# Two graph-attention and mixture-of-experts layers on one core: where the second early fetch of sums and the first early stores stand in SyncE's queue

## The chip, the cores and the metric

The kernel runs on one core of one Trainium2 chip. The metric is the device time of one execution in microseconds (us); lower is better. Times are medians of several executions. A profile is one further execution, taken by the hardware profiler[...].

Engines are named as in the profile: PE is TensorE, DVE is VectorE, ACT is ScalarE, POOL is GpSimd, SP is SyncE. A letter q behind an engine's name means its sequencer, which issues DMAs, waits on semaphores and takes branches. Each engine works through its own instructions in order. A block, below, is a page of 128 token rows that belong to one expert.

## The reference

The input is `x` (2708 rows of 256 numbers) and an adjacency matrix `adj` (2708 x 2708). There are two layers, each an attention over the graph and then a mixture of experts, both added to their input. What matters here is the very end, the mixture of experts of layer 1:

```python
def _L1_ffn_ref(x, gate_w, gate_b, w1, b1, w2, b2, gamma, beta):
    B, S, H, F, E, K = (8, 4096, 256, 512, 16, 2)
    gate_logits = x @ gate_w + gate_b
    topk_vals, topk_idx = jax.lax.top_k(gate_logits, K)
    topk_w = jax.nn.softmax(topk_vals, axis=-1)
    h = jax.nn.relu(jnp.einsum('bsh,ehf->bsef', x, w1) + b1)
    expert_out = jnp.einsum('bsef,efh->bseh', h, w2) + b2
    sel = jnp.take_along_axis(expert_out, topk_idx[:, :, :, None], axis=2)
    moe = jnp.sum(topk_w[..., None] * sel, axis=2)
    y = x + moe
    ...
    return (y - mu) / jnp.sqrt(var + EPS) * gamma + beta
# layer 1, last step
x = x + _L1_ffn_ref(_layernorm(x)[None], ...)[0]
```

Every row goes to 2 of 16 experts. The two results are weighed, summed with the row, normalised, and added to the layer's input.

## The kernel before

**Tiles and blocks.** The 2708 rows lie in 22 tiles, tiles 0 to 19 of 128 rows and two of 74 rows at the end. For the experts the rows are sorted into blocks. Layer 1 has 45 blocks that are certain to be needed (`SURE1`, numbers 0 to 44) and up to 13 more that stand in a branch, `rest()`, which is taken only if the routing needs them. It is not taken with this input.

**One block** is computed by `Experts.stream`. Its steps, with the lines of the profile:

- `load_w1` (L749) and `load_w2` (L753): SP issues the two weight transfers of the block's expert, 512 KB each. There are three rooms for weights, and block b uses room b % 3: the tiles named `wide_mask` are rooms 0 and 1, the tile named `room` is room 2. A transfer is left out when the room already holds the expert. Such an issue still waits like any other, but takes about 0.08 us in SP's timeline instead of 0.38.
- `fetch` (L765): SP issues the load of the block's 128 rows into `xr`.
- `turn` (L461) and the copy to `lo` (ACT, L1007): the rows are transposed.
- `hide` (PE, L880, 8 matrix products in 16 records) fills `hid_ps` from w1; `bend` (ACT, L884, 4 times) applies the relu into `ht`.
- `weigh`: DVE forms `side` (L872), ACT forms the weight `w` (L874).
- `sum_hidden` (PE, L898) fills `out_ps` from `ht` and w2; PE does it for block b after `hide` of block b+1.
- `scaled` (DVE, L902 and L904) multiplies by the weight into `yo`; `add` (POOL, L909) is an indirect DMA that adds the rows onto `sums1[b % 2]` in DRAM. An add waits until the last add on the same half has landed.

**The end of a tile.** When its two sums are complete, they are fetched from `sums1` into `y_all` (the profile calls it `mask_t`, whose room it uses), added, normalised and stored. For tiles 0 to 11 this is done early, beside the last blocks, by `early_last`: the fetch of six tiles from both halves (SP, L1417, two transfers of 768 KB), three additions (POOL, L1947), statistics (DVE, L427 and L428), the reciprocal root (DVE, L368 to L380) and two operations a tile (DVE, L1957 and L1959). Tiles 0 to 5 are ready once blocks below 36 are added, tiles 6 to 11 once blocks below 39 are.

**After the blocks**, all engines come to the branch of `rest()` (L940 and L943). On the path that skips it each sequencer waits for what its engine has issued and then raises the semaphores that the skipped work would have raised; POOL's entry of this kind is `INC_SWDGE_SEM`. Only then can SP issue the fetches of the ten last tiles (`load_y`, L1417 and L1420, eight transfers), because they wait for those semaphores. Then come the stores of tiles 0 to 11 (L2039), and `last1` finishes tiles 12 to 21 (L1981 on PE, L427, L434, L452, L2001, L2005) with their stores (L2007, L2013).

**What sets the order.** Within this stage a planner, `Clock`, runs generator pieces against assumed durations. A piece yields an engine and a time, or a `Mark` that it waits for, and the order in which pieces are resumed is the order in which instructions are written into each engine's queue. `clock.moved` sets a mark from an assumed time of a transfer; `clock.set` sets it to now. The pieces `fetcher` (issues L765) and `loader` (issues L749 and L753) run through all 45 blocks. The planner's times are not the chip's: an instruction that is written early and whose semaphore comes late holds all that stands behind it.

Of the kernel before, what the change touches and what calls it, by code (L numbers as in the profile page):

```python
# [146 lines left out]
def kernel(  # L147
# [25 lines left out]
    nc = tc.nc  # L173
# [11 lines left out]
    tiles = [(t, P if t < TF else TAIL) for t in range(T)]  # L185
# [90 lines left out]
    def of_pair(src, lo, r=P):  # L276

        return src[lo * P:lo * P + 2 * r, :].rearrange("(p s) d -> p s d", s=2)
# [434 lines left out]
    class Experts:  # L713
# [236 lines left out]
        def stream(self, clock, stages, bank, acc, xrs, los, wides, widened, started):  # L950

            NB, FC = self.sure, self.FC
            self.known_at, self.planned_at, self.scattered_at = (
                {upto: Mark() for upto in stages} for _ in range(3))
            self.added_at = [Mark() for _ in range(NB)]
            hidden_at, out_at, xg_at, xt_at, ht_at, w_at = (
                [Mark() for _ in range(NB)] for _ in range(6))
            xr_slots, xts, weights, hidden = {}, {}, {}, {}
            hts = Slots(clock, 2)

            def stage(b):
                return next(upto for upto in stages if b < upto)

            def fetcher():
                for b in range(NB):
                    yield self.known_at[stage(b)]
                    yield self.scattered_at[stage(b)]
                    if b >= 3:
                        yield hidden_at[b - 3]
                    xr_slots[b] = yield from xrs.get()  # L970
                    self.fetch(b)
                    clock.moved(xg_at[b], 0.5, 2.2)

            def loader():
                yield widened
                for b in range(NB):
                    yield self.known_at[stage(b)]
                    if b < 2:
                        room = []
                        for _ in range(2):  # L980
                            yield from wides.get()
                            room.append(wide_tile())
                        self.add_room(b, *room)
                    else:
                        yield started
                        yield hidden_at[b - 2]
                    self.choose(b)
                    self.load_w1(b)
                    clock.moved(Mark(), 1.7, 2.0)
                    if b >= 3:  # L990
                        yield out_at[b - 3]
                    self.load_w2(b)
                    clock.moved(w_at[b], 1.7, 2.0)

            def turn(b):
                yield xg_at[b]
                slot = yield from bank.get()
                ps = ps_tile("tr_ps", self.t_tag)[:, :D].rearrange("p (c n) -> p c n", n=P)
                yield "PE", 0.4
                turn_rows(self.rows[b][:, :D], P, ps)  # L1000
                clock.start(turned(b, ps, slot), 0)

            def turned(b, ps, slot):
                lo_slot = yield from los.get()
                xt = self.xt_tile()
                yield "ACT", 0.4
                nc.scalar.copy(xt, ps)  # L1007
                clock.set(slot)
                xts[b] = xt, lo_slot
                clock.set(xt_at[b])  # L1010

            def relu(b, f, ps, slot):
                yield "ACT", 0.38
                self.bend(b, f, hidden[b][0], ps)
                clock.set(slot)
                if f == FC - 1:
                    clock.set(ht_at[b])

            def weigh(b):
                yield "DVE", 0.2  # L1020
                yield "ACT", 0.3
                weights[b] = self.weigh(b)

            def finish(b, ps, slot):
                yield "DVE", 0.7
                yo = self.scaled(b, ps, weights.pop(b))
                clock.set(slot)
                yield "POOL", 1.6
                self.add(b, yo)
                clock.set(xr_slots.pop(b))  # L1030
                clock.set(self.added_at[b], 4.5)

            def outputs(b):
                slot = yield from acc.get()
                ps = ps_tile("out_ps", self.o_tag)
                yield ht_at[b]
                yield "PE", 2.05
                ht, ht_slot = hidden.pop(b)
                self.sum_hidden(b, ht, ps)
                clock.set(ht_slot)  # L1040
                clock.set(out_at[b])
                clock.start(finish(b, ps, slot), 0)

            def compute():
                yield started
                yield from turn(0)
                due = []
                for b in range(NB):
                    yield self.planned_at[stage(b)]
                    yield xt_at[b]  # L1050
                    yield w_at[b]
                    slot = yield from hts.get()
                    hidden[b] = self.pool.tile([P, FC, P], F32, name="ht", bufs=2), slot
                    xt, lo_slot = xts.pop(b)
                    clock.start(weigh(b), 0)
                    for f in range(FC):
                        slot = yield from bank.get()
                        ps = ps_tile("hid_ps", self.h_tag)
                        yield "PE", 0.47
                        self.hide(b, f, xt, ps)  # L1060
                        clock.start(relu(b, f, ps, slot), 0)
                        if f == 0:
                            clock.set(hidden_at[b])
                    clock.set(lo_slot)
                    due.append(b)
                    if b + 1 < NB:
                        there = xg_at[b + 1].at is not None and xg_at[b + 1].at <= clock.now
                        if there:
                            yield from turn(b + 1)
                        while len(due) > there:  # L1070
                            yield from outputs(due.pop(0))
                        if not there:
                            yield from turn(b + 1)
                    self.beside(b)
                for b in due:
                    yield from outputs(b)

            clock.start(fetcher())
            clock.start(loader())
            clock.start(compute(), 2)  # L1080

# [571 lines left out]
    for k in range(17):  # L1653
# [8 lines left out]
        if k >= 14:  # L1662
            lo = 4 * (k - 14)
# [37 lines left out]
    clock = Clock()  # L1701
# [14 lines left out]
    def small(n):  # L1716

        return "DVE", 0.19 * n
# [202 lines left out]
    def add_to_x(t, r):  # L1921
# [5 lines left out]
    y_all = mask_flat.bitcast(F32)[:, :2 * T * D].rearrange(  # L1927
        "p (k t d) -> p k t d", k=2, d=D)
# [5 lines left out]
    EARLY_LAST = ((tiles[:6], 36), (tiles[6:12], 39))  # L1934
    assert ENDS1[:2] == (6, 12) and list(early1.values()) == [8, 20] and E1 == 16

    def early_last(group, done):

        yield experts1.added_at[done - 1]
        mark, lo, n = Mark(), group[0][0], len(group)  # L1940
        for k in range(2):
            experts1.early_read(k, fetch_rows(y_all[:, k, lo:lo + n], sums1[k], group), done)
        clock.moved(mark, 0.8 * n, 2.5)
        yield mark
        for t in range(lo, lo + n, 2):
            yield "POOL", 1.3
            nc.gpsimd.tensor_tensor(y_all[:, 0, t:t + 2], y_all[:, 0, t:t + 2],  # L1947
                                    y_all[:, 1, t:t + 2], OP.add)
        for t, r in group:
            yield "DVE", 0.63  # L1950
            ln_y.stats(y_all[:, 0, t], t, r)
        yield small(13)
        rsqrt(ts(ln_y.mv[:, lo:lo + n, 1], LN_EPS, OP.add), ln_y.rstd[:, lo:lo + n])
        for t, r in group:
            yield "DVE", 0.95
            y = y_all[:, 1, t]
            nc.vector.scalar_tensor_tensor(y, y_all[:, 0, t], ln_y.mv[:, t, 0:1], last["gamma"],  # L1957
                                           op0=OP.subtract, op1=OP.mult)
            nc.vector.scalar_tensor_tensor(y, y, ln_y.rstd[:, t:t + 1], x1[:, t, :], op0=OP.mult,  # L1959
                                           op1=OP.add)  # L1960

    def load_y(group, mark):
        lo = group[0][0]
# [65 lines left out]
    clock = Clock()  # L2029
# [4 lines left out]
    loads = [Mark() for _ in late_last]  # L2034
    for group, mark in zip(late_last, loads):
        load_y(group, mark)
    for group, _ in EARLY_LAST:
        for (t, _), _ in zip(group[::2], group[1::2]):
            nc.sync.dma_start(of_pair(out, t), y_all[:, 1, t:t + 2])  # L2039
    for group, mark in zip(late_last, loads):  # L2040
        clock.start(last1(group, mark))
    clock.run()
# [31 lines left out]
```

## Time and profile before

| | |
|---|---|
| Median of 3 runs | 1165.3 us (1164.83 to 1167.05) |
| Profiled execution, its own time | 1183.92 us |
| Its span, first to last instruction | 1182.2 us |
| PE busy | 1049.9 us, 89% of the span |
| DVE, ACT, POOL busy | 537.3, 575.6, 367.1 us |
| Mean granted PE clock | 0.944 |
| Moved by DMA | 238.96 MB, 202 GB/s on average |

PE is busy in nearly the whole span, but the 40 slices of the page (29.6 us each) show it at 8, 5 and 3 tenths in the last three: the end of the kernel is a stage with limits of its own. It is this end, from about 1095 us on, that the change touches; so it is read from the timeline, the stages and the chain of that stretch, and not from the busy shares of the whole. "Idle before, and its releaser" in a timeline names the event that came last before the instruction could start.

### The profile page before, as it was taken

To read this page: it belongs to the slowest core of one execution; us is meant where nothing else is said; L and a number is where in the kernel's file an instruction comes from. 1 tells how busy PE (TensorE), PEld (TensorE's weight loads), DVE (VectorE), ACT (ScalarE), POOL (GpSimd) and SP (SyncE) were. 2 spreads that over 40 slices of the span, in tenths; PEclk is the share of its full clock that TensorE was granted. 3 is DMA by queue.
4 is the path that set the end of the run, shared out by engine and by line. 5 is a ranking of instruction groups with operands and counts; after the bars stand their busy time and mean duration, and the time that the engine had idled before them with its cause. 6 is when DMAs were issued, how large, how long until landed. Compare 5 with 4: busy or idle time off the path is not lost. (4 is left out here: it accounts for less than half of the span.)

```text
span 1182.2 us, 21323 instructions
## 1 busy us (share of the span) xinstructions
PE 1049.9 (89%) x6705; PEld 928.9 (79%) x6705; DVE 537.3 (45%) x2073; ACT 575.6 (49%) x1609; POOL 367.1 (31%) x422
## 2 busy tenths in 40 slices
PE   5999999969989999999998999998865698899853
PEld 4888888857879999989998746998865587898742
DVE  7778888856521111110111357367755631122454
ACT  4877677644534444434444475457544244344312
POOL 7611121211242222221224330542540635333432
PEclk9999999988999999999999999998976899899966
DMA  9964554312879999999899689001315457778943
GB/s 282 303 233 147 169 168 150 134 70 66 302 229 317 322 324 323 320 284 331 265 317 363 189 240 285 1 6 50 104 50 181 123 142 180 181 200 206 302 107 120
DMA packets 165053, 238.96 MB, mean 202 GB/s; under 512 B 10627, under 2 KB 139966, under 8 KB 162224
## 3 DMA queue, kind: packets, MB, share of 16 engines
q1 hardware_dynamic: 146116, 214.09, 55.2%
q0 software_dynamic: 18816, 23.42, 10.4%
q8 instruction: 56, 0.92, 0.3%
q14 instruction: 65, 0.53, 0.2%
HBM read 205.54 MB, written 54.99 MB: 220 GB/s over the span
## 5 line engine op out<-in xcount | busy, mean ns | idle before, releaser
L904 DVE TENSOR_SCALAR yo<-out_ps,w 128x256 f32<-128x256 f32 x92 | 44.5, 484 | 416.1 <-PE out_ps L898 408.0
L1235 PE MATMUL att_ps<-g_all,z 128*128 128x257 f32 (+3 forms) x968 | 227.2, 388 | 0.0
L1235 PEld LDWEIGHTS att_ps<-g_all,z 128*128 128x128 f32 (+3 forms) x968 | 177.3, 188 | 36.3 <-issue 9.0
L898 PE MATMUL out_ps<-room,ht 128*128 128x256 f32 x872 | 199.0, 380 | 0.0
L880 PEld LDWEIGHTS hid_ps<-xt,room 128*128 128x128 f32 x1504 | 175.3, 192 | 10.9 <-ACT w L874 4.2
L880 PE MATMUL hid_ps<-xt,room 128*128 128x128 f32 x1504 | 177.3, 276 | 7.1 <-DMA room<-in_L_ffn_W_dram 3.8
L898 PEld LDWEIGHTS out_ps<-room,ht 128*128 128x128 f32 x872 | 161.3, 191 | 20.8
L1221 ACT ACTIVATE zr<-e_bc,minus_one,g_all 128x256 f32<-128x256 f32 (+3 forms) x242 | 130.5, 592 | 58.6 <-DVE z L1224 57.9
L884 ACT ACTIVATE ht<-hid_ps,w_t 128x128 f32<-128x128 f32 x376 | 128.4, 364 | 30.8 <-PE hid_ps L880 8.2
L909 POOL DMA_INDIRECT sums<-yo,xg x43 | 66.9, 1556 | 234.2 <-DVE side L872 178.3
L1635 PE MATMUL att_ps<-half,wide_mask 128*128 128x258 f32 (+1 forms) x968 | 127.0, 293 | 3.9 <-issue 2.4
L674 POOL DMA_INDIRECT rows_d<-xr,place x88 | 91.9, 1044 | 123.7 <-DVE xr L443 77.0
L1635 PEld LDWEIGHTS att_ps<-half,wide_mask 128*128 128x128 f32 (+1 forms) x968 | 124.0, 198 | 5.0 <-issue 2.5
L909 POOL DMA_INDIRECT sums<-yo,xr x45 | 70.7, 1571 | 143.5 <-DMA sums<-yo,xr 37.0
L1224 DVE SCALAR_TENSOR_TENSOR z<-zr,mask_t 128x256 f32<-128x256 f32 (+3 forms) x242 | 96.0, 419 | 30.4 <-ACT zr L1221 16.8
L884 ACT ACTIVATE ht<-hid_ps,w1x 128x128 f32<-128x128 f32 x180 | 61.3, 362 | 97.7 <-PE hid_ps L880 82.0
L874 ACT ACTIVATE w<-xg,side 128x1 f32<-128x1 f32 x43 | 12.7, 294 | 165.9 <-DVE side L872 165.9
L880 PE MATMUL hid_ps<-lo,wide_mask 128*128 128x128 f32 x480 | 67.3, 298 | 15.2 <-DMA wide_mask<-in_L_ffn_w_dram 13.7
L880 PEld LDWEIGHTS hid_ps<-lo,wide_mask 128*128 128x128 f32 x480 | 64.5, 211 | 19.3 <-issue 15.5
L1512 POOL CAST wide_mask<-mask_t 128x1408 fp32r<-128x1408 fp8e4 x31 | 42.6, 1376 | 104.8 <-PE att_ps L1635 70.7
L898 PE MATMUL out_ps<-wide_mask,ht 128*128 128x256 f32 x240 | 61.3, 401 | 0.0
L461 PE MATMUL tr_ps<-ident,xr 128*128 128x128 f32 (+1 forms) x214 | 38.8, 290 | 23.9 <-DMA xr<-rows_d 9.0
(296 smaller groups left out, 1355.7 us busy)
## 6 DMA issues: line engine op xcount, KB each, us to landing
room<-in_L_ffn_W_dram SPq DMA_DIRECT2D x94, 1024.0 KB
wide_mask<-in_L_ffn_w_dram SPq DMA_DIRECT2D x60, 512.0 KB
room<-in_adj_dram SPq DMA_DIRECT2D x20, 1354.0 KB
room<-in_L_ffn_w_dram SPq DMA_DIRECT2D x30, 512.0 KB
rows_d<-nobody SPq DMA_DIRECT2D x1, 7511.0 KB
rows_d<-nobody SPq DMA_DIRECT2D x5, 1295.0 KB
sums<-nobody SPq DMA_DIRECT2D x2, 2944.0 KB
xr<-rows_d SPq DMA_DIRECT2D x45, 129.5 KB
```

Of the source, the lines that this page charges most:

```text
L461: nc.tensor.transpose(ps[:, c, :r], src[:, c * P:(c + 1) * P], ident[:r, :r])
L674: ins = nc.gpsimd.indirect_dma_start(out=self.rows_d[:, :], in_=self.rows[t][:r], in_offset=None, out_offset=bass.IndirectOffsetOnAxis(ap= ...
L880: nc.tensor.matmul(ps[:, :P], w1_b[:, c, f * P:(f + 1) * P], xt[:, c, :], start=(c == 0), stop=(c == DC - 1))
L884: nc.scalar.activation(ht[:, f, :], ps[:, :P], self.func, bias=self.bias[:, f, b:b + 1])
L898: nc.tensor.matmul(ps[:, :D], ht[:, f, :], self.rooms[b % 3][1][:, f, :], start=False, stop=(f == self.FC - 1))
L904: nc.vector.tensor_scalar(yo, ps[:, :D], w, None, op0=OP.mult)
L909: ins = nc.gpsimd.indirect_dma_start(out=self.sums[k][:, :], in_=yo, in_offset=None, out_offset=bass.IndirectOffsetOnAxis(ap=self.rows.pop ...
L1221: nc.scalar.activation(zr[:k, :n], e_bc[:k, lo:lo + n], AF.Relu, bias=minus_one[:k], scale=g_all[:k, j, D + 1:D + 2])
L1224: nc.vector.scalar_tensor_tensor(z[:k, :n], zr[:k, :n], 1.0, mask_t[:k, j // 2, lo:lo + n, j % 2], op0=OP.add, op1=OP.mult)
L1235: nc.tensor.matmul(accs[i][:r, :D + 1], z[:k, q * P:q * P + r], g_all[:k, j, :D + 1], start=(j == 0), stop=(j == LAST))
L1512: nc.gpsimd.tensor_copy(m, src)
L1635: nc.tensor.matmul(accs[i][:, :D + 2], wide_masks[i, j % 2][:k, j // 2, :], half_k[:k, j, :], start=(j == 0 and half_k is halves[0]), stop ...
```

## The change

The fetch of tiles 6 to 11 waits, in the planner, for two new marks: `loaded`, set when the loader has issued the weights of the last block, and `fetched`, set when the fetcher has issued the rows of the last block. The fetch of tiles 0 to 5 stays where it was. Tiles 0 to 5 are stored by the same piece that finishes them, which also waits for the two marks before it issues the three stores; the stores of tiles 6 to 11 stay behind the branch.

```diff
@@ Experts.stream
             self.added_at = [Mark() for _ in range(NB)]
+            self.loaded, self.fetched = Mark(), Mark()
@@ fetcher
                     self.fetch(b)
                     clock.moved(xg_at[b], 0.5, 2.2)
+                clock.set(self.fetched)
@@ loader
                     self.load_w2(b)
                     clock.moved(w_at[b], 1.7, 2.0)
+                clock.set(self.loaded)
@@ early_last(group, done)
         yield experts1.added_at[done - 1]
         mark, lo, n = Mark(), group[0][0], len(group)
+        if lo:
+            yield experts1.loaded
+            yield experts1.fetched
         for k in range(2):
             experts1.early_read(k, fetch_rows(y_all[:, k, lo:lo + n], sums1[k], group), done)
         clock.moved(mark, 0.8 * n, 2.5)
...
             nc.vector.scalar_tensor_tensor(y, y, ln_y.rstd[:, t:t + 1], x1[:, t, :], op0=OP.mult,
                                            op1=OP.add)
+        if not lo:
+            yield experts1.loaded
+            yield experts1.fetched
+            early_out(group)
+
+    def early_out(group):
+        for (t, _), _ in zip(group[::2], group[1::2]):
+            nc.sync.dma_start(of_pair(out, t), y_all[:, 1, t:t + 2])
@@ after the branch
     for group, mark in zip(late_last, loads):
         load_y(group, mark)
-    for group, _ in EARLY_LAST:
-        for (t, _), _ in zip(group[::2], group[1::2]):
-            nc.sync.dma_start(of_pair(out, t), y_all[:, 1, t:t + 2])
+    early_out(tiles[6:12])
```

In the program that comes out of the planner, PE's order is the same as before. The other queues, from the fetch on:

- SP, before: w1 of block 42; fetch of tiles 6 to 11; w2 of 42; rows of 44; w1 and w2 of 43; w1 and w2 of 44; branch; eight late fetches; six stores.
- SP, after: w1 and w2 of 42; rows of 44; w1 and w2 of 43; w1 and w2 of 44; fetch of tiles 6 to 11; three stores; branch; eight late fetches; three stores.
- POOL, before: the additions of tiles 6 to 11 stand between the adds of blocks 40 and 41. After: they stand behind the add of block 44, ahead of the branch.
- DVE, before: statistics, root and final operations of tiles 6 to 11 stand among `yo` of blocks 41 to 44. After: all of them stand behind `yo` of block 44, ahead of the branch. `side` of block 42 stands ahead of the final operations of tile 0 instead of behind those of tile 1.
- ACT: `w` of block 42 stands behind the copy to `lo` of block 43, where it stood ahead of three of the relus of block 42.

## The prediction

> **What bounds the kernel now.** I read the end of the kernel backwards. The chain of work that ended last gives the points that everything hangs on (columns: start, us, what):
>
> ```profile
> 1119.48 26.52 DMA sums<-yo,xr
> ...
> 1146.07 0.39 SPq L1417
> ...
> 1149.54 12.30 DMA mask_t<-sums
> ...
> 1161.89 5.46 PE y_ps L1981 x14
> ```
>
> The first late fetch leaves at F = 1146.07. Behind it the stage is a fixed piece: 12.3 us until the 74-row fetch lands, then products, roots and stores, 36.1 us in all to the span's end at 1182.2. The 26.5 us in front are put down to one add, but they hide the path I need, so I asked for SP's timeline and for that of the engines. SP:
>
> ```profile
> 1110.61 0.37 SPq L749 DMA_DIRECT2D wide_mask<-in_L_ffn_w_dram  x1
> 1113.18 0.96 SPq L1417 DMA_DIRECT2D mask_t<-sums  x2
> 1114.55 0.54 SPq L753 DMA_DIRECT2D wide_mask<-in_L_ffn_w_dram  x1
> ...
> 1118.32 0.38 SPq L749 DMA_DIRECT2D wide_mask<-in_L_ffn_w_dram  x1
> ```
>
> w1 of block 42 at 1110.61, then the fetch of tiles 6 to 11, which waits for the adds of blocks 37 and 38 until 1113.18, then w2 of 42, and only at 1118.32 w1 of block 43. The engines (in brackets: idle before, and who ended it):
>
> ```profile
> 1117.91 1.89 PE L898 MATMUL out_ps<-room,ht 128*128 128x256 f32 x8
> ...
> 1126.68 3.75 PE L880 MATMUL hid_ps<-lo,wide_mask 128*128 128x128 f32 x16 [6.88 <-DMA wide_mask<-in_L_ffn_w_dram]
> ...
> 1133.28 1.95 PE L880 MATMUL hid_ps<-lo,room 128*128 128x128 f32 x16
> ...
> 1137.02 1.89 PE L898 MATMUL out_ps<-room,ht 128*128 128x256 f32 x8
> ...
> 1140.67 1.55 POOL L909 DMA_INDIRECT sums<-yo,xr  x1 [0.91 <-DVE yo L904]
> ```
>
> PE stands 6.88 us before block 43, for that w1. The same 16 records then take 3.75 us instead of 1.95, since the granted clock is 0.50 from 1122 to 1132 (stages of 2 us). So PE loses 6.9 us by the wait, and about 2.8 more by the clock: block 44 starts 6.60 us after block 43, where undisturbed blocks follow each other at 3.84 (1103.49, 1107.34, 1111.18). The last add starts at A = 1140.67, and F follows 5.40 us later. What fills these is in the rows of the branch:
>
> ```profile
> L943 POOLq INC_SWDGE_SEM  x1: 1596/1596/1596, 1144.5 to 1144.5; - x1
> ```
>
> The add lands about 3.8 us after its start, POOL's sequencer then spends 1.6 us raising the semaphores of the work skipped, and SP goes.
>
> [...] w1 of 43, issued 4.2 us behind 1.5 MB of sums and 3.8 behind w2 of 42, landed after 8.3 us. [...] L1957 takes 1.48 us beside POOL's L1947, 0.48 without. [...] the add at 1127.46 does start just when the additions end.
>
> **The change, part by part.**
>
> *The fetch goes behind the weights.* SP is freed of a wait (until 1113.18) and of two issues (0.96). w2 of 42 then waits only for `out_ps` of block 39 (PE done at 1111.34): 1111.4. Steps of SP as now (1.3 us to the rows, 1.8 to the next w1) give rows of 44 at 1112.7 and **w1 of 43 at 1114.5**, 3.8 us earlier, with 0.5 MB of w2 ahead of it instead of 2 MB. Block 38's w1, behind a full queue, took 6.1 us (1091.81 to 1097.9); in a queue that is nearly drained (131 GB/s in 1114 to 1116, 278 before) I estimate 4 to 5: landed by 1119.2. PE is free at 1119.8.
>
> *PE also needs `lo` of 43.* Before, ACT stood at `w` of 42 until DVE reached `side` at 1121.34, so `lo` came at 1122.9; a block 43 with early weights would still have lost 3 us. In the new order that `w` stands behind `lo`, so `lo` is there at about 1118.6. Block 43 starts at **1119.9**.
>
> *From there to the last add.* DVE is busy with tiles 0 to 5 (six times 0.91 us from 1119.7, with L902 and L904 of block 41, 0.64, and two `side`): `side` of 43 at 1123.1, so ACT ends `w` and the last relu of 43 at 1123.9 and `lo` of 44 at 1124.3. Block 44 starts at 1124.4, then 1.95 + 1.85 + 1.9 for itself and two `out_ps`: PE ends at 1130.1 instead of 1138.9. DVE has nothing else queued there (tiles 6 to 11 stand behind), so `yo` starts at 1130.1, and **A = 1130.9** (0.77 us after `yo`, as now). The add of 42, which it must wait for, starts at 1127.0 and lands at 1130.8. A comes 9.8 us earlier.
>
> *The fetch itself* (two issues, 1.5 MB) waits behind w2 of 44, and that for `out_ps` of 41, 1119.8: issued by 1121.0. It took 9 us to its first use before (1114.1 to 1123.15), in a fuller queue; so 1130 at the latest. The first user, POOL, is not free before A + 1.55 = 1132.5. Nothing stands behind it on SP but stores and the branch: no cost.
>
> *Three stores ahead of the branch.* They wait for DVE to end tile 5, 1126, cost SP 3 x 0.4 us, and their 768 KB land by about 1131. SP's part of the branch waits for them, but F comes later. Cost nothing, under cover of the adds; without it 2 to 3 us. Three stores fewer behind F gain nothing: the chain there hangs on the 74-row fetches, at 49 GB/s and a DMA share of 0.13 (1155 to 1157), two of 16 engines; the stores queue behind them.
>
> *Three additions of POOL move between the last add and the branch.* They took 4.15 us before; from A + 1.55 they end at A + 5.75. Does `INC_SWDGE_SEM` wait for them? The trace doesn't show this case. Lower bound: it does not, and F = A + 5.4; a gain is excluded, since nothing leaves POOL's path there. Upper bound: it does, and F = A + 5.75 + 1.6 + 0.1 = A + 7.45. Indirect DMAs do queue behind additions, so I take the upper one: F = 1130.9 + 7.45 = **1138.4, 7.7 us earlier**. Against it: in layer 0 the same operation (started 673.5, 1.49 us) ran beside an add that occupied POOL until 674.4.
>
> *DVE's work on tiles 6 to 11* now follows the additions: 0.53 a tile for statistics, 2.4 for the root, 12 x 0.47 for L1957 and L1959; it ends at about A + 15 = 1146, and holds up the late statistics, which would start 6.9 us after F, at 1145.3. That costs about a microsecond there, hidden: DVE had stood 6.4 us before the 74-row tile (until 1164.76, 18.7 us after F). If the cover were gone it would be 1 to 2.7 us.
>
> **Sum.** 9.8 - 2.1 = 7.7 us. Profiled execution: 1183.9 - 7.7 = 1176.2 us. It stands 18.6 us above the median of the runs (1.6%); the gain is waiting for DMA and PE at half clock, so I take it over unscaled: 1165.3 - 7.7 = **1157.6 us**.
>
> **The rivals.**
> - *POOL's semaphores don't wait for the additions*: all 9.8 us arrive, 1155.5. For it: the overlap in layer 0. [...]
> - *The weights of 43 are late again*: at 8.2 us after issue, as before, they land at 1122.7. PE idles 2.9 us and runs one block at half clock (3.59 instead of 1.95, as after the 1.93 us gap at 1096.0). 4.5 us of the gain go: 1162.1.
> - *Nothing is gained*: something else, the adds' own succession or DVE, holds A to within 2 us of now. Against it: adds of both halves are 3.8 us apart and land in 3.8.
> - *Slower*: POOL becomes the end. The additions run beside DVE's statistics and take the longest value seen, 1.86 us each; then F = A + 1.55 + 5.6 + 1.6 = A + 8.8, 3.4 us worse than now. It decides as soon as A comes forward by less than 3.4 us; with no gain in A, 1168.7. Against it: 6.9 us of idle PE are plain, and what ended them is moved.
> - That the change doesn't do what it says is excluded: the new queue has the weights ahead of the fetch.
>
> **How the numbers follow.** Forecast 0.47; semaphores pass 0.27; weights late 0.12; no gain 0.07; slower 0.07. About 0.2% (2.3 us) is what a measurement of this kernel can tell from no change. The first three lie beyond it: faster 0.86, same 0.08, slower 0.06 (a small part of the slow case lies within). The range goes from 1154.3 (all 9.8 and a microsecond of steps that run closer than I put them) to 1162.2 (weights late).
>
> **What would show it.** In the profile after: no wait of PE for `wide_mask` near block 43, or one under 1 us; clock 1.00 through blocks 43 and 44; w1 of 43 on SP about 3.8 us behind w1 of 42; the last add some 10 us earlier; POOL's L1947 behind it, and the first late fetch 7.4 us after it (5.4 if the semaphores pass); 36 us from there to the end. I am wrong if PE still waits over 2 us there, if the last add moves by less than 5 us, or if the stage behind F gets longer because DVE comes late.

## The result and the profile after

The median fell from 1165.07 us (20 runs) to 1159.62 us (20 runs, 1152.76 to 1166.44). The ratio is 0.9954 with a 95% interval of 0.9932 to 0.9975, that is 5.4 us, between 2.9 and 7.9. Two later sets of runs gave 0.9952 (0.9934 to 0.9971) and 0.9939 (0.9918 to 0.9960). The gain is real; it is somewhat smaller than the 7.7 us of the forecast. Of the executions reported below one, of the kernel with the fetch alone, took 1562.73 us at a granted clock of 0.647; its median and ratio leave that one out.

The profiled execution took 1164.64 us with a span of 1162.9, so the two spans differ by 19.3 us. Most of that has nothing to do with the change: block 38, ahead of everything the change touches, already starts 12.7 us earlier. One profile is one execution. So I compare stages, counted from the start of block 42 on PE, and not ends. A wait just ahead of that point is left out by this, and the first profile of after has one, for w1 of block 41:

```profile
1099.05 3.27 PE L880 MATMUL hid_ps<-lo,room 128*128 128x128 f32 x16 [2.10 <-DMA room<-in_L_ffn_w_dram]
```

The profile of before has no such wait. It is not the stall in a new place, though: waits of 1.0 to 2.4 us ahead of block 41 stand in nine of the fourteen profiles of this document, two of them of kernels with the fetch at its old place.

SP's timeline of the kernel after shows w1 of blocks 42 and 43 (the first two lines), the moved fetch and the three stores:

```profile
1096.22 0.37 SPq L749 DMA_DIRECT2D wide_mask<-in_L_ffn_w_dram  x1
...
1100.12 0.37 SPq L749 DMA_DIRECT2D wide_mask<-in_L_ffn_w_dram  x1
...
1108.78 0.96 SPq L1420 DMA_DIRECT2D mask_t<-sums  x2
1109.85 4.15 SPq L1974 DMA_DIRECT2D out_dram<-mask_t  x3
```

w1 of 43 goes out 3.9 us behind w1 of 42; it was 7.7 us before. In the engines' timeline of the kernel after, blocks 43 and 44 start 3.84 us apart with no wait, at full clock (1.00 from 1103.00 to 1120.07; 1.95 us each):

```profile
1108.45 1.95 PE L880 MATMUL hid_ps<-lo,wide_mask 128*128 128x128 f32 x16
...
1112.29 1.95 PE L880 MATMUL hid_ps<-lo,room 128*128 128x128 f32 x16
...
1114.56 1.54 POOL L909 DMA_INDIRECT sums<-yo,xr  x1 [2.88 <-DVE w L902]
...
1117.95 0.48 DVE L904 TENSOR_SCALAR yo<-out_ps,w 128x256 f32<-128x256 f32 x1 [1.29 <-PE out_ps L898]
1118.12 1.55 POOL L909 DMA_INDIRECT sums<-yo,xr  x1 [2.01 <-issue]
1121.91 1.54 POOL L909 DMA_INDIRECT sums<-yo,xr  x1 [2.25 <-issue]
1122.91 4.27 POOL L1953 TENSOR_TENSOR mask_t<-mask_t 128x512 f32<-128x512 f32 x3
```

The stall is gone. What is new stands in the last four lines: `yo` of 44 starts at 1117.95, but the add that takes it only at 1121.91, 3.96 us later, where it was 0.77. The timeline puts that idle time down to "issue", which names no cause. In the program, this add waits for the landing of the add of block 42 on the same half of the sums. The wait itself is on record with POOL's sequencer (duration in ns: least, median, most; first and last start in us), which stands at a semaphore of L909 from 1117.9 for 3.31 us:

```profile
L909 POOLq EVENT_SEMAPHORE  x1: 3310/3310/3310, 1117.9 to 1117.9; - x1
```

In the trace the landing of an add is 16 updates of its semaphore. Those of the add of block 42 (started at 1114.56) come from 1119.68 to 1121.19, the last 6.6 us behind its start; the sequencer's wait ends at 1121.2 and the last add starts 0.72 us behind the landing. Likewise 43 waits for 41 (1110.13, landed at 1117.39 after 7.3 us) and starts 0.72 us behind it. In the fourteen profiles together, 18 of the adds of blocks 41 to 44 start 0.72 us behind the landing of the add before them on their half: these are the adds that were held by it.

The branch's row for POOL's sequencer in the kernel after (columns as above):

```profile
L943 POOLq INC_SWDGE_SEM  x1: 1596/1596/1596, 1125.5 to 1125.5; - x1
```

POOL's sequencer begins to raise the semaphores at 1125.5, while the three additions of POOL (1122.91 + 4.27) still run until 1127.2. What it waited for is the last add: the raising starts 0.02 to 0.03 us behind the landing of that add in all fourteen profiles. The first late fetch leaves at 1127.13, 5.22 us behind the last add.

Followed back from the end, the chain of work that ended last now reaches no further than this (second line: PE on the late tiles):

```profile
1136.47 0.24 issue
1136.71 5.59 PE y_ps L1995 x16
```

and PE's timeline says what it had waited for:

```profile
1136.71 10.77 PE L1995 MATMUL y_ps<-mask_t,ident 128*128 128x256 f32 x40 [18.79 <-DVEq L943]
```

Before, PE began on the late tiles 3.0 us behind the first late fetch and then stood for the 74-row fetches. Now it begins 9.6 us behind it, because DVE, which has the statistics and the twelve final operations of tiles 6 to 11 ahead of the branch, reaches the branch only at 1136.2. From there PE never stops. The stage behind the fetch is 35.8 us, where it was 36.1: the same length, with another cause.

The stages of every profile (one execution each), in us. The first two columns go from start to start of blocks 42, 43 and 44 on PE; A is the last add, F the first late fetch. The kernels of the experiments are described below.

| Kernel | 42 to 43 | 43 to 44 | 44 to `yo` of 44 | `yo` to A | A to F | F to end | 42 to end |
|---|---|---|---|---|---|---|---|
| before | 10.99 | 6.60 | 6.62 | 0.77 | 5.40 | 36.1 | 66.5 |
| after | 3.84 | 3.84 | 5.66 | 3.96 | 5.22 | 35.8 | 58.3 |
| after, second | 3.92 | 3.99 | 5.77 | 3.58 | 5.43 | 35.9 | 58.6 |
| after, third | 3.86 | 4.04 | 5.77 | 3.44 | 5.25 | 36.3 | 58.7 |
| fetch alone | 3.95 | 4.50 | 5.77 | 3.31 | 5.33 | 35.7 | 58.5 |
| stores alone | 11.74 | 6.15 | 6.62 | 0.76 | 5.39 | 34.1 | 64.7 |
| behind w1, stores early | 6.21 | 5.56 | 5.67 | 0.77 | 5.39 | 36.2 | 59.8 |
| behind w1, stores late | 3.84 | 4.05 | 5.77 | 2.17 | 5.27 | 35.4 | 56.5 |
| the same, second | 3.85 | 4.09 | 6.51 | 1.08 | 5.43 | 35.3 | 56.2 |
| the same, third | 3.84 | 4.20 | 6.63 | 1.27 | 5.32 | 35.7 | 57.0 |
| after, an eighth of the bytes | 3.98 | 4.45 | 5.77 | 1.89 | 5.35 | 35.3 | 56.8 |
| before, an eighth | 10.39 | 6.30 | 6.61 | 0.76 | 5.36 | 34.3 | 63.7 |
| engines' order alone | 10.29 | 5.78 | 5.66 | 0.78 | 5.74 | 35.2 | 63.5 |
| engines' order, an eighth | 7.16 | 5.27 | 5.66 | 3.60 | 5.25 | 36.2 | 63.1 |

### The profile page after: what moved, and what is told of

Read it like the earlier page. It is cut to its first block, busy times and chain, and to the rows that moved or that the text cites. A ratio compares the mean times of both kernels' runs of the same rounds, so it can differ in the third digit from the quotient of the medians.

```text
span 1162.9 us, 21320 instructions
## 1 busy us (share of the span) xinstructions
PE 1042.8 (90%) x6705; PEld 925.1 (80%) x6705; DVE 537.8 (46%) x2073; ACT 577.9 (50%) x1609; POOL 367.4 (32%) x422
## 5 line engine op out<-in xcount | busy, mean ns | idle before, releaser
L1224 ACT ACTIVATE zr<-e_bc,minus_one,g_all 128x256 f32<-128x256 f32 (+3 forms) x242 | 130.4, 592 | 58.8 <-DVE z L1227 58.1
L909 POOL DMA_INDIRECT sums<-yo,xg x43 | 66.8, 1554 | 233.9 <-DVE side L872 185.3
L909 POOL DMA_INDIRECT sums<-yo,xr x45 | 70.8, 1574 | 128.6 <-DMA sums<-yo,xr 40.8
L874 ACT ACTIVATE w<-xg,side 128x1 f32<-128x1 f32 x43 | 12.7, 294 | 169.1 <-DVE side L872 169.1
```

The source lines that it names most:

```text
L909: ins = nc.gpsimd.indirect_dma_start(out=self.sums[k][:, :], in_=yo, in_offset=None, out_offset=bass.IndirectOffsetOnAxis(ap=self.rows.pop ...
L1224: nc.scalar.activation(zr[:k, :n], e_bc[:k, lo:lo + n], AF.Relu, bias=minus_one[:k], scale=g_all[:k, j, D + 1:D + 2])
```

## The experiments

They were run in three sets; within a set all kernels and the kernel before ran on the same chip, and only these are compared. The kernel before took 1186.40, 1183.55 and 1164.71 us in the three.

### Which part of the change does it

Fetch alone: the fetch of tiles 6 to 11 is moved, all six early stores stay behind the branch.

```diff
-        if not lo:
-            yield experts1.loaded
-            yield experts1.fetched
-            early_out(group)
...
-    early_out(tiles[6:12])
+    early_out(tiles[:12])
```

> The fetch of tiles 6 to 11 moved as in the changed kernel, all six early stores behind the branch as before. Theory (the moved transfers slow the last adds): the 1.5 MB of sums alone still lie ahead of the adds of blocks 41 and 42, so these land in 5.5 to 7.3 us instead of 3.8; the last add starts 11.5 to 13.5 us behind the start of block 43's hidden products (13.5 in the changed kernel, 10.2 if nothing slowed the adds); time 1157.5 to 1160. Rival (the adds are late for POOL's or DVE's own order): nothing moves, 13.5 us and 1159.6. Second rival (the stores are the harm): adds land in 3.8 us, 10.2 us, 1156.4.

Measured: 1181.46 us, ratio 0.9956 (0.9937 to 0.9975), the gain of the whole change. The last add starts 13.6 us behind block 43. That rules out the second rival, that the stores are the harm, but it doesn't tell the theory (up to 13.5) from the first rival (13.5); this is settled further down.

Stores alone: the fetch stays, the stores of tiles 0 to 5 go ahead of the branch.

```diff
-        if lo:
-            yield experts1.loaded
-            yield experts1.fetched
         for k in range(2):
             experts1.early_read(k, fetch_rows(...), done)
```

> The fetch of tiles 6 to 11 stays at its old place, only the three stores of tiles 0 to 5 go ahead of the branch. Theory: PE's wait of 5 to 7 us before block 43 is back with its half clock behind it, the last add lands in 3.8 us, and the time is that of before, 1164 to 1166. Rival (the three stores carry the gain [...]): 1159 to 1161, and the 74-row fetch lands earlier than 15.8 us behind the first late fetch.

Measured: 1186.43 us, ratio 1.0003 (0.9981 to 1.0025). PE's timeline of this kernel has the stall back, and the last add lands in 3.8 us again:

```profile
1128.83 3.75 PE L880 MATMUL hid_ps<-lo,wide_mask 128*128 128x128 f32 x16 [7.74 <-DMA wide_mask<-in_L_ffn_w_dram]
```

So the gain is the fetch's; the three stores give and cost nothing that can be told from zero (2.3 us under to 3.0 over).

### Does the fetch have to go behind all weights?

Behind w1: the fetch stands behind w1 of block 43 and ahead of its w2; the additions are kept behind all adds. Once with the three stores ahead of the branch, once with all six behind it.

```diff
@@ loader
                     clock.moved(...)
+                    if b == NB - 2:
+                        clock.set(self.w1_out)
@@ early_last
         if lo:
-            yield experts1.loaded
-            yield experts1.fetched
+            yield experts1.w1_out
         for k in range(2):
             experts1.early_read(k, fetch_rows(...), done)
+        if lo:
+            yield experts1.loaded
+            yield experts1.fetched
```

> As the changed kernel, with the orders of PE, DVE, ACT and POOL unchanged; on SP the fetch of tiles 6 to 11 stands behind w1 of block 43 instead of behind w2 of 44. Theory: w1 of 43 is still in time (no wait of PE over 1 us before block 43), the 1.5 MB are through before the adds of 41 to 43 start, these land in 3.8 to 5 us, the last add starts 10.2 to 11 us behind block 43's start instead of 13.5, time 1156 to 1157.5. Rival (POOL's or DVE's own order): 13.5 us and 1159.6 as in the changed kernel. Against both: w2 of 43, now behind the fetch, comes late for its products, PE waits before them, and the time is 1160 to 1163.

> As the kernel with the fetch behind w1 of block 43, and all six early stores behind the branch. Theory: adds land in 3.8 us [...], the last add 10.2 us behind block 43's start, time 1155.5 to 1157. If the stores cost the adds nothing, the same as with them; if they cost 1 us of landing, 1 us below it. Rival (POOL's or DVE's order): 13.5 us, 1159.6.

Measured: 1179.43 us, ratio 0.9940 (0.9915 to 0.9965), and 1178.88 us, ratio 0.9941 (0.9915 to 0.9966). In the first one's profile PE stood 2.1 us ahead of block 43: w1 of 43, with 1.5 MB issued 0.6 us behind it, took 7.3 us to land. It did not stand there in any of the three profiles of the second, where w1 landed in 4.8 to 5.1 us with the same bytes behind it. What made the difference is open. (PE had waited 1.0 to 1.5 us ahead of block 41 in these three and only 0.1 in the first, so SP was further ahead of it by 0.5 to 1.0 us.) The last add waits less in these kernels than in the kernel after (`yo` to A 0.8 to 2.2 us). It stands 12.0 us behind block 43 in both, less than the rivals' 13.5 but more than the theories' 10.2 to 11.

The second form again, beside the kernel after, in two more sets:

> The changed kernel once more, beside the three kernels that run with it on the same chip. Both theories: some 5.4 us under the kernel before (ratio 0.9932 to 0.9975); last add 13 to 13.6 us behind the start of block 43, because the adds of 43 and 44 wait for the landing of the adds of 41 and 42, 7 to 8 us after their start; semaphores raised beside the additions, first late fetch 5.2 to 5.4 us behind the last add.

> The fetch of tiles 6 to 11 behind w1 of block 43, ahead of its w2, all six early stores behind the branch; once more, beside the changed kernel. If the place of the fetch behind w1 is what matters, it lies 1 to 3 us under the changed kernel, since the 1.5 MB of sums have passed before the adds of 42 to 44: last add 10.8 to 12 us behind the start of block 43. Rival: the two are alike, the weights of 44 pay for it (w2 of 43 behind 1.5 MB holds up PE by what the adds save), within 1 us of each other.

> The fetch behind w1 of 43, ahead of its w2, all early stores behind the branch, beside the changed kernel once more. If its place is the better one, 1 to 3 us under the changed kernel again (it was 1.9 under it, with intervals that meet); if the two are alike, within 1 us.

> The changed kernel on the same chip, for the comparison with the fetch behind w1: 5 to 6 us under the kernel before.

Measured: 1177.55 (after) and 1175.69 us (behind w1; ratio to before 0.9931, 0.9912 to 0.9949) in one set, 1158.06 and 1156.07 us (0.9917, 0.9887 to 0.9947; 6 runs) in the other. It was 1.9 and 2.0 us lower. Each pair's intervals meet; both pairs together, resampled, give 1.9 us with a 95% interval that begins at zero (0.0 to 3.8). The kernel after did not run in the first set; there this version lies 2.6 us under the fetch alone, with an interval of 2.3 over to 4.4 under. PE's timeline of the last run shows what it pays:

```profile
1105.85 1.99 PE L899 MATMUL out_ps<-wide_mask,ht 128*128 128x256 f32 x8 [0.60 <-DMA wide_mask<-in_L_ffn_w_dram]
```

In this profile w2 of 43, now behind the 1.5 MB, holds PE 0.6 us (44 to `yo` is 6.6 instead of 5.8), and the adds give back 2.2 (`yo` to A 1.27 instead of 3.44). Of the versions that do all the work this one is probably the best, by 2 us.

### Why the last adds land late

The kernel after with the moved fetch cut to 16 of 128 rows:

```diff
+            if lo:
+                ins = nc.sync.dma_start(y_all[:16, k, lo:lo + n], <rows 0 to 15 of each tile>)
+            else:
+                ins = fetch_rows(y_all[:, k, lo:lo + n], sums1[k], group)
```

> The changed kernel, but the fetch of tiles 6 to 11 brings only 16 of the 128 rows of each tile, an eighth of its bytes, in the same two issues with the same waits (the remaining rows of these tiles are left out). Theory, the 1.5 MB delay the landing of the adds: the adds of 41 and 42 land within 4.5 us, those of 43 and 44 start within 1 us of their yo, the last add stands 10.3 to 11 us behind the start of block 43, and the time is 2 to 3.2 us under the changed kernel. Rival, the order on POOL or DVE (or the three stores, 0.75 MB) sets them: the last add stays 13 us or more behind it and the time within 0.8 us of the changed kernel.

Measured: 1173.48 us (6 runs; ratio 0.9912, 0.9880 to 0.9944), 4.1 us under the kernel after in the same set (1.5 to 8.2; 2 to 3.2 were expected). The last three adds in POOL's timeline:

```profile
1128.61 1.55 POOL L909 DMA_INDIRECT sums<-yo,xr  x1 [2.88 <-DVE w L902]
1130.54 1.55 POOL L909 DMA_INDIRECT sums<-yo,xr  x1 [0.38 <-DVE w L902]
1133.51 1.55 POOL L909 DMA_INDIRECT sums<-yo,xr  x1 [1.43 <-issue]
```

The adds of 42 and 43 now start 0.76 us behind their `yo`, so those of 40 and 41 have landed in time: in about 4.5 and 3.6 us, where they took 8.4 and 7.8 in the second profile of after. The last one still starts 1.89 us behind its `yo`: 42 took 4.2 us to land, 0.72 follow until the next add starts, and `yo` of 42 and 44 are only 3.8 us apart. DVE and POOL have the same order as in the kernel after, so it is not their order that delays the adds of 40 and 41. Of the 3.6 us in the second profile of after the bytes are the cause of about 1.7 (one profile of each); 0.8 are there in the kernel before too, and the remaining 1.1 are the adds' own succession. The last add stood 12.1 us behind block 43, between the two expectations (11 at most, 13 at least).

The third profile of after has both kinds of landing within 12 us: of the adds of 40 and 41 (first line), and of those of 42 and 43, which start when the sums have landed:

```profile
DMA to landing us min/median/max: 7.9/8.2/8.5
DMA to landing us min/median/max: 4.0/4.0/4.1
```

The traffic, in stages of 2 us (the last three columns are PE's clock, the DMA share and GB/s), for the kernel after:

```profile
1112.00:1114.00 2.00, 2.00 (x19) 1.95 (x18) 1.83 (x6) 0.91 (x3) 0.00 (x0) 1.00 1.10 341
1114.00:1116.00 2.00, 2.00 (x13) 1.68 (x12) 0.46 (x3) 1.10 (x4) 1.44 (x1) 1.00 1.07 296
1116.00:1118.00 2.00, 1.92 (x10) 1.35 (x8) 0.59 (x3) 0.93 (x1) 0.10 (x1) 1.00 1.11 347
```

and with an eighth:

```profile
1123.00:1125.00 2.00, 2.00 (x14) 1.83 (x14) 1.87 (x7) 0.39 (x2) 1.07 (x2) 1.00 0.90 147
1125.00:1127.00 2.00, 1.64 (x13) 1.23 (x12) 1.93 (x5) 1.14 (x4) 0.73 (x1) 1.00 0.72 165
```

In the kernel after the adds of 41 and 42 are under way from 1110.1 to 1121.2, and from 1112 to 1118 the DMA share is 1.07 to 1.11, at 296 to 347 GB/s. How the adds and the sums divide the DMA engines between them no run here shows. The adds' own packets in the trace of after show where the time goes: the first packet of the add of 41 starts 5.3 us behind the add, and the last one ends 1.7 us later; of the last add these are 2.1 and 1.1 us. Of the 3.4 us by which the add of 41 lands later than that of 43 (7.26 against 3.88), 3.1 lie ahead of the first packet (5.25 against 2.13). Why there, stays open.

### What made the stall: the queue of SP, the bytes, or the order of the engines

The kernel before, its fetch at the old place but with an eighth of the bytes (the same edit on the kernel before):

> The kernel before, with the fetch of tiles 6 to 11 at its old place but only an eighth of its bytes (16 of 128 rows of each tile; the rest is left out). SP still waits there for the adds of 37 and 38, so w1 of 43 is issued as late as before, but with 0.7 instead of 2 MB ahead of it. Theory, the wait and the order of issue make the stall: PE still stands 5 us or more ahead of block 43 and the time is within 2 us of the kernel before. Rival, the bytes ahead of w1 make it: w1 lands some 4 us after its issue, PE stands 3 us or less (for lo of 43, which still comes late), and the time falls by 4 to 6 us.

Measured: 1183.48 us, ratio 1.0014 (0.9993 to 1.0035). Nothing was gained, and PE stood as the theory had it, but neither theory had named the reason. The timeline of the engines in this kernel:

```profile
1121.98 5.00 DVE L1963 SCALAR_TENSOR_TENSOR mask_t<-mask_t,mv_y,gamma 128x256 f32<-128x256 f32 x1
...
1127.67 0.29 ACT L874 ACTIVATE w<-xr,side 128x1 f32<-128x1 f32 x1 [7.93 <-DVE side L872]
...
1128.62 0.38 ACT L1007 COPY lo<-tr_ps 128x256 f32<-128x256 f32 x1
...
1129.05 3.78 PE L880 MATMUL hid_ps<-lo,wide_mask 128*128 128x128 f32 x16 [6.38 <-ACT lo L1007]
```

PE stands 6.38 us again, but it is `lo` that ends the wait (1129.00); of the 16 marks of w1's landing the trace has 12, the last of these at 1123.8. The short fetch lands early, so POOL starts its additions at 1122.43; one operation of DVE with two inputs in SBUF, 0.48 us otherwise, then takes 5.00 us and ends at 1126.98, 0.3 us behind the third of three additions in a row (1126.70). (In the profile of before operations of this kind took 0.84 to 1.48 us beside the additions; these 5.00 us are the longest in the traces.) Behind it stand `side` of 42, ACT's `w` of 42, and `lo` of 43. So block 43 had two conditions that came late. In the kernel before, too, `lo` came late, at 1122.9, 3 us after PE was free; the bytes taken away brought the additions forward and made that second wait longer.

Engines' order alone: the planner is told to fetch at the old place and to work on the tiles late. DVE and ACT come out in the order of the fetch moved alone, SP in that of before; POOL's three additions stand between the adds of 40 and 42. The six stores are moved behind the branch as in the fetch alone; that part of the edit is left out here.

```diff
-        if lo:
-            yield experts1.loaded
-            yield experts1.fetched
         for k in range(2):
             experts1.early_read(k, fetch_rows(...), done)
+        if lo:
+            yield experts1.loaded
+            yield experts1.fetched
```

> The fetch of tiles 6 to 11 at its place of before on SP, but DVE and ACT in the order of the kernel with the fetch moved (lo of 43 ahead of w of 42; the work on tiles 6 to 11 behind the last yo), all early stores behind the branch; POOL's three additions stand between the adds of 40 and 42. Theory, SP's queue makes the stall and the engines' order only a second wait behind it: w1 of 43 is as late as before, PE stands 5 us or more ahead of block 43 for wide_mask, lo of 43 is there 4 us or more before it, and the time is within 2 us of the kernel before. Rival, the engines' order makes it (in the kernel before with an eighth of the bytes it was lo that ended the wait): PE stands 3 us or less and the time falls by 4 us or more.

Measured: 1162.54 us, ratio 0.9976 (0.9957 to 0.9995): 2.2 us gained, 4.5 us (2.1 to 7.2) above the kernel after. Its timeline:

```profile
1099.47 0.37 ACT L1010 COPY lo<-tr_ps 128x256 f32<-128x256 f32 x1
...
1099.96 0.38 SPq L749 DMA_DIRECT2D wide_mask<-in_L_ffn_w_dram  x1
...
1107.40 3.75 PE L880 MATMUL hid_ps<-lo,wide_mask 128*128 128x128 f32 x16 [6.18 <-DMA wide_mask<-in_L_ffn_w_dram]
```

`lo` of 43 is there 8 us early, and PE still stands 6.18 us for w1, which lands 7.3 us after its issue. SP's queue made the stall, as the first theory had it; the time fell by slightly more than the 2 us that it allowed. The 2.2 us are found in the table behind the stall. 44 to `yo` is 1.0 us shorter than before, since the work of DVE on tiles 6 to 11 no longer stands between the last `yo` (before, PE ended at 1138.9 and `yo` of 44 started at 1139.90). 43 to 44 is 0.8 us shorter for another reason, the clock: the `out_ps` that starts 4.1 to 4.2 us behind the start of block 43 took 1.89 us in this profile, as at full clock, and 2.58 in that of before, where the clock stood at 0.50 until 5.6 us behind that start.

The same with an eighth of the bytes:

> As the one with the engines' order alone, but the fetch at its old place brings an eighth of the bytes (16 of 128 rows of each tile; the rest is left out). Now SP's wait is left without the bytes and without the late lo. Theory, wait and bytes make half each: w1 of 43 is issued about 4 us late and lands about 4.5 us later, PE stands 2 to 4 us, and the time falls by 3 to 6 us. Rival A, the wait alone: PE stands 5 us or more, within 2 us of the kernel before. Rival B, the bytes alone: PE stands under 1 us and the time falls by 7 us or more.

Measured: 1161.87 us, ratio 0.9971 (0.9952 to 0.9991), 0.7 us under the one with all bytes (2.9 under to 2.3 over). Its timeline:

```profile
1106.05 3.38 PE L880 MATMUL hid_ps<-lo,wide_mask 128*128 128x128 f32 x16 [3.04 <-DMA wide_mask<-in_L_ffn_w_dram]
...
1108.44 3.70 DVE L1969 SCALAR_TENSOR_TENSOR mask_t<-mask_t,mv_y,gamma 128x256 f32<-128x256 f32 x1
...
1108.79 3.05 POOL L1959 TENSOR_TENSOR mask_t<-mask_t 128x512 f32<-128x512 f32 x2
...
1114.65 0.48 DVE L904 TENSOR_SCALAR yo<-out_ps,w 128x256 f32<-128x256 f32 x1
```

w1 (issued 1101.82) lands in 4.1 us instead of 7.3, and the stall is 3.04 us instead of 6.18. So of the stall, with `lo` early, half is the late issue and half the bytes ahead of it: the theory of half and half, as far as the stall goes. For the time it missed (3 to 6 us expected, 2.8 measured, hardly more than with all bytes): one operation of DVE takes 3.70 us beside two additions of POOL and ends 0.3 us behind them, `yo` of 42 comes at 1114.65 though PE was done with its block at about 1111.5, and the last add has to wait for the landing of that block's add (`yo` to A 3.60 us). What PE won, the adds lost.

## Why the prediction was right, and where it was off

The direction, the mechanism of the gain and the range held (1159.6 in 1154.3 to 1162.2); the size was 2.3 us too good. Inside the sum two terms were wrong by about 2 us each, with opposite signs.

- **The fetch goes behind the weights, and `lo` of 43.** Right, both. Block 43 follows 42 by 3.84 us (4.2 in the forecast), and 44 follows 43 by 3.84 to 4.04 (4.5). The experiments held PE for 6.2 us by late weights with `lo` early, and for 6.4 us by a late `lo` with a light fetch, so the change had to bring both forward, and does. The rival of late weights did not happen: PE waits for no weights there in any of the three profiles of after. The margin is thin: w1 of 43 landed 1.9, 0.9 and 0.1 us ahead of the block's start.
- **From there to the last add.** This is the term that was mis-sized. `yo` of 44 came as early as reckoned or earlier, but the add behind it was put 0.77 us later and stands 3.4 to 4.0 us later. From block 42 to A the forecast has 15.2 us, the three profiles 17.1 to 17.3. The step took an add's landing of 3.8 us from a stretch in which the DMA engines had little else to do (71 GB/s, the adds themselves); the adds of 40 to 42 took 6.0 to 8.5 us there, except for those of 42 in the second and third profile (4.1 and 4.0). It also let the last add start 0.1 us behind the landing it waits for, and that step takes 0.72.
- **The fetch itself: "no cost".** Wrong, and the same error from the other side. I asked who waits for the fetch and who stands behind it on SP, and found nobody. But the 1.5 MB are moved into the very stretch in which the last adds land (DMA share 1.07 to 1.11 from 1112 to 1118 in the first profile of after). Cutting the bytes to an eighth took 1.7 us from this wait. The price stood in the trace of before: by their landing marks the adds of 39 and 40, beside the same fetch at its old place, took 9.25 and 7.32 us.
- **Three stores ahead of the branch: nothing.** Right (ratio 1.0003), although SP is at them for 4.15 us, waits included, where 1.2 were reckoned; F came 13 us after they were out.
- **Three additions of POOL.** The upper bound was chosen and the lower one is true: in every profile with the additions behind the last add F comes 5.2 to 5.4 us behind it. This made F some 2.1 us earlier than the forecast, from A. The rival "semaphores don't wait" was right on its mechanism and wrong as a whole, because the adds took its gain away.
- **DVE's work on tiles 6 to 11: hidden.** Nearly. The stage behind F did not get longer than in the profile of before, but its cover is used up: the chain of the kernel after hangs on DVE's arrival at the branch, no longer on the 74-row fetches. The two other profiles of kernels that run as long as before have 34.1 and 34.3 us there, against 35.8 to 36.3 in the three of after, so perhaps 1 us is paid, inside the 1 to 2.7 that were named for this case. No run took this work away by itself.
- **Two readings of the trace.** The 12.3 us to the landing of the 74-row fetch count from that fetch's own issue; from F it is 15.8. And the half clock did not need the 6.88 us: it began at 1122.0, 2.2 us after PE stopped. From block 38 on, a block ran slower behind gaps of PE of 1.9 to 2.4 us in eight cases (its 16 records took 2.63 to 3.59 us; in the profiles of before and after the clock stood at 0.50 for 3.41 us, behind gaps of 1.93 and 2.10), and behind gaps of 1.9 to 2.5 us in five others it did not (2.02 us). What decides between them these traces do not show.

In the profiles the two errors nearly cancel: block 42 to the end was forecast at 58.8 us and measured 58.3 to 58.7. That it came so close is luck. That the medians show 5.4 to 6.7 us and not 7.7 I put to the point of comparison: the profile of before has 66.5 us in this stage, and the two kernels that tie with it (stores alone, before with an eighth) 64.7 and 63.7. The mean of the three, 65.0, less 58.5 is 6.5 us. (Counted from block 38, with the waits ahead of block 41 in it, the same six profiles give 83.1 less 76.3, 6.8 us.) That one profiled execution overstated the stall by a microsecond or two is an argument from three profiles, not a measurement.

## What to carry to other kernels

When a transfer is moved out of somebody's way, ask not only who waits for it and who stands behind it in its queue, but whose DMAs are in flight where it arrives: a landing time measured in a quiet stretch (3.8 us here) didn't hold beside 1.5 MB (6.0 to 8.5 us). The trace of before may have the price already, where the same two ran side by side. Before crediting a stall to the event that ended it, look for the next condition of the same instruction; here weights and `lo` were both late, and with one alone made earlier PE still stood over 6 us. And a gain at the end of a kernel should be counted from a common point inside it, in more than one profile of the kernel before.

## What the hardware showed

- The last add, an indirect DMA, lands 3.6 to 4.1 us behind its start in the fourteen profiles. Beside the fetch of sums the adds of 40 and 41 took 6.0 to 8.5 us in the three profiles of the kernel after, and that of 40 took 8.66 with the fetch alone. The first packet of the add of 41 starts 5.3 us behind the add in the first profile of after, where it is 2.1 us for the last add.
- An add that is held by the landing of another starts 0.72 us behind it (18 cases).
- POOL's sequencer raises the skipped work's semaphores (1.6 us) while POOL's own additions still run (from 1125.53 in the first profile of after, with the additions until 1127.18), although an add that stands behind additions does wait for them (in the profile of before the additions end at 1127.30 and the add of 41 starts at 1127.46). The raising starts 0.02 to 0.03 us behind the landing of the last add.
- An operation of DVE with two SBUF inputs that meets additions of POOL took up to 5.00 us instead of 0.48: that one ended only behind the third of three additions in a row.
- A w1 transfer of 512 KB with 1.5 MB issued 0.5 to 0.6 us behind it took 7.3 us in one profile and 4.8 to 5.1 in three others: the place in the queue alone did not settle when it landed.
